# A graph layer on one core: the last two adjacency tiles loaded by row groups, zero products in TensorE's gaps, roots on VectorE, and a new split of PSUM banks

## The chip, the cores and the metric

The kernel runs on one core of a Trainium2 chip. Its time is the device time in microseconds; the median of the runs counts. Profiles are of one execution each, and every time inside one is counted from the start of its span. PE is TensorE, DVE is VectorE, ACT is ScalarE, POOL is GpSimd, and SP is the queue that issues the transfers.

## The reference

`x` is 4096 by 64, `adj` is a 4096 by 4096 matrix of zeros and ones in float32 (64 MB), `weight` is 64 by 64 and `bias` has 64 values.

```
h       = relu(layernorm(x))
support = h @ weight
mask    = adj != 0
rank    = cumsum(mask, axis=1)
deg     = rank[:, -1:]
k       = minimum(deg, 100)
pos     = rank - (deg - k)
w       = mask * where(pos > 0, 0.5 ** (k - pos), 0)
out     = x + w @ support + bias
```

Only a row's last hundred neighbours count, and each weighs half of the next one. So every row needs a running count over its 4096 columns before its weights are known.

## The kernel before

`adj` is worked through in 32 tiles of 128 rows, each 2 MB. Thirty are loaded whole as "rows" (line 307, in units of two tiles): a partition holds one row of 4096 floats in a run of 16 KB. Tile 0 comes in two halves. Tiles 30 and 31 form one unit of kind "columns": a partition holds a quarter of the columns of four rows, so that four row groups and four column quarters are spread over the partitions, and the runs are 4 KB. Tile 31 is two pieces of 128 columns there. Each of the quarter's transfers goes to 32 partitions (line 311):

```
to = tiles[t].rearrange("(q p) (g n) -> q p g n", q=E, g=E)
for q in range(E):
    nc.sync.dma_start(to[q, :, k0:k1, :], quarters[t // HT, t % HT, q, :, k0:k1, :])
```

Each piece passes these steps. `convert` (DVE, line 509) turns floats into bytes, `flip` (DVE, lines 520 and 525) transposes blocks of them, `totals` (PE, 532) counts ones, `split` (ACT, 538) takes two bytes of the counts, `suffix` (PE, 551) adds up what lies behind each block, `clamp` (DVE, 556) subtracts the excess over 100, `place` (PE, 565 and 570) writes into four PSUM banks the exponent of every element, and four `weigh` (ACT, 584) take the exponentials, which are the weights. `aggregate` (PE, 601) multiplies them with the support, 32 products for a unit of two tiles. After each four tiles `drain` (ACT, 611; the last one DVE, 613) adds the bias, `turn_back` (PE, 619) transposes, `finish` (DVE, 626 and 627) adds the two halves to `x`, and `store` (SP, 631) writes out.

Ahead of that stands the layer norm: `turn`, `turned`, `center`, `square`, `relu`, `spread` (PE, 458), `root` (DVE, 462 to 464), `power` (POOL, 469 to 474, three Newton steps for the reciprocal root), `support` (PE, 479), `scale` (DVE, 482), `first` and `second` (ACT and DVE, 489 and 492), which split the support into two summands.

The order on every engine is fixed before the kernel runs. `tasks` lists each step with the engine, what it needs, how long it holds its engine, and a due time from the table `DUE`. `plan` then walks through the tasks and gives each engine's next one by readiness and due time; the kernel issues them in that order, and every engine keeps it. So an engine that stands at a step that isn't ready holds back all behind it. A load of tile t waits for the convert of tile t - 4, since there are four buffers for loaded tiles (`NA`). There are four for converted bytes (`NM`) and four for flipped ones (`NT`).

PSUM's eight banks are divided in `NV, NB`: five for exponents (pool `ps_v`, also used by the layer norm), two for counts (pool `ps_t`: totals, suffix and turn_back take turns), and one for the accumulator (`ps_a`).

`warm` issues products of zeros, which keep PE at work in early gaps. It is called from the loop at the end of the kernel, from line 637 on, where the plan leaves PE idle for more than 700 ns, and no more once `spread` has come.

Of the kernel before, what the change touches and what calls it, by code (L numbers as in the profile page):

```python
# [30 lines left out]
UNITS = [("rows", ((t, 0, 4), (t + 1, 0, 4))) for t in range(0, 30, 2)] + [("columns", ((30, 0, 4), (31, 0, 2), (31, 2, 4)))]  # L31
SPANS = {"rows": 8, "columns": 2}
STEP = {0: 2}
# [3 lines left out]
for u, i in PIECES:  # L37
# [3 lines left out]
DRAINS = [(g, 0, 4, True) for g in range(7)] + [(7, 0, 2, True), (7, 2, 3, True), (7, 3, 4, False)]  # L41
STORES = [(0, 0, 16), (1, 0, 12), (1, 12, 14), (1, 14, 15), (1, 15, 16)]
NA, NM, NT, NW, NV, NB = 4, 4, 4, 2, 5, 2

DUE = {
    "fetch": [-686, -126],
    "load": [724, 583, 273, 792, 448, 655, 939, 650, 1013, 730, -119, 964, 1305, 584, 218, 814, 1129, 955, 149, 993, 40,
    765, 956, 78, 684, 958, 306, 922, 424, 450, 164, 71, 1115, 730],
    "load_rest": [-204],
    "turn": [359, 315, 260, 710, 487, 222, 133, -266],  # L50
    "turned": [-185, -335, 64, -727, -1045, -251, -968, -881],
    "center": [360, -58, 207, -35],
    "square": [-87, -1268, -175, 619],
    "relu": [-239, 514, 1391, -334],
    "spread": [-680, -580, -580, 15],
    "support": [21, 24, 95, 42],
    "scale": [861, -308, -468, -124],
    "root": [844],
    "power": [174],
    "constants": [-220, -1059],  # L60
    "order_of": [1056],
    "count": [1111],
    "counted": [10],
    "first": [-514, -397, -30, -113],
    "second": [-417, 143, 783, 704],
    "convert": [482, 1025, 204, 226, 727, 309, 981, 1114, 367, 687, 1132, 1067, 867, 1749, 1371, 1701, 256, 1583, 1540,
    856, 1257, 1456, 1412, 1612, 1915, 1541, 2485, 1819, 1871, 2184, 1807, 1638, 1616, 2086],
    "flip": [-114, 308, 291, 923, 674, -114, 690, 807, -100, 831, 543, 437, 630, 1887, 1255, 1800, 979, 1228, 961, 744,
    1153, 1971, 1323, 1552, 1990, 1126, 1724, 1289, 2088, 1984, 2223, 1296, 1905, 2123],
    "totals": [-3, 552, -46, 841, 433, 189, 81, 601, 415, -464, -591, 136, 611, 1280, 503, 1008, 578, 335, 987, 424,  # L70
    685, 602, 1305, -158, 1197, 1439, 1190, 839, 1469, 919, 1061, 1251, 1091],
    "split": [761, 727, 1045, 717, 751, 769, -156, 772, 17, 1132, 865, 862, 499, 667, 955, 987, 1510, 1187, 1234, 350,
    1194, 1337, 750, 878, 1289, 1830, 1061, 1369, 1498, 1532, 1176, 1109, 1727],
    "suffix": [183, 405, -150, 111, 631, -317, 930, 770, 128, 167, 1286, 587, 1533, 512, 1005, 852, 704, 676, 956, 1751,
    1680, 1362, 1491, 577, 1388, 1268, 1495, 1814, 1765, 1130, 1431, 1709, 2042],
    "clamp": [321, 347, 443, 415, 222, 598, 567, 424, 121, 506, 857, 749, 466, 653, 638, 701, 1299, 997, 674, -57, 972,
    1295, 1419, 477, 1910, 863, 1576, 1079, 584, 801, 1235, 1277, 1913],
    "place": [-25, 778, 16, 550, 117, -32, 40, -6, 92, 41, -143, 48, 468, -231, -158, 1140, 356, 68, 498, 801, 768,
    1322, 971, 1992, 893, 1057, 834, 1829, 1233, 1823, 1881, 1472, 1293],
    "weigh": [-539, -10, 974, 122, -11, -72, 83, 150, 27, 775, 317, 129, -832, -333, -51, 636, 535, 294, 532, 123, 180,  # L80
    378, 466, -70, 639, 222, 730, 838, 795, 370, 3, 64, 752, 536, 729, 774, 139, 88, 559, 654, 785, 582, 88, 787, 1053,
    118, 807, 706, 489, 825, 591, 69, 761, 655, 427, 704, 340, 743, -9, 457, 789, 281, 1115, 479, 792, 1172, 665, 313,
    1129, 1711, 790, 1140, 1070, 953, 1054, 509, 1453, 384, 1493, 842, 315, 782, 467, 940, 983, 1433, 1265, 954, 1411,
    876, 1666, 1502, 1255, 848, 803, 1220, 1400, 1237, 1021, 1867, 1311, 858, 1342, 1376, 1740, 1425, 1760, 1471, 2210,
    1505, 1441, 1561, 1791, 1838, 1656, 2274, 2036, 1458, 1383, 852, 799, 1464, 848, 1978, 1179, 1428, 1547, 1352, 796,
    2201, 1653, 1588],
    "aggregate": [405, 292, 97, 611, -155, 1241, -31, 842, 332, 334, 1114, 914, 1063, 882, 706, 826, 632, 748, 1116,
    423, 423, 679, 89, 819, 525, 722, 392, 807, 611, 1238, 1392, -269, 1280, 824, 135, 740, 1044, 980, 682, 959, 368,
    650, 826, 977, 447, 432, 945, 564, 860, 911, 943, 1550, 795, 1481, 1191, 503, 690, 693, 824, 516, 1094, 676, 1580,
    2035, 1092, 1330, 876, 1281, 1390, 1259, 1542, 2317, 1637, 1016, 1566, 1168, 1392, 1083, 962, 1526, 1048, 1123,  # L90
    1190, 1017, 661, 1207, 2606, 1891, 1494, 1205, 1663, 1458, 782, 2062, 1503, 2022, 1500, 2071, 2003, 1841, 1219,
    1977, 1613, 827, 1835, 2025, 1748, 1355, 1745, 1953, 2096, 2431, 899, 2009, 1570, 1701, 1819, 1985, 2681, 1641,
    1109, 2260, 2265, 2409, 2272, 1848, 924, 1875],
    "drain": [64, 247, 512, 1185, 1142, 1625, 1534, 1794, 1955, 2201],
    "turn_back": [1333, 1555, 2261, 2462, 2286, 2762, 2419, 1952, 2550, 2777],
    "finish": [403, 912, 821, 1212, 1760, 2467, 1688, 2395, 2803, 2383],
    "store": [10242, 11508, 11343, 11289, 10767],
# [14 lines left out]
def tasks():  # L112
# [36 lines left out]
    task("power", (), POOL, 3, 2600, 2700, [("root",)])  # L149
# [8 lines left out]
    for n, (u, i, k0, k1) in enumerate(LOADS):  # L158
        k = k1 - k0
        due = when[u, i]  # L160
        hold = 622 * k + 20
        task("convert", (n,), DVE, due, hold, hold + 170, [("load", n)], ("b", ("flip", n)))
        hold = 268 * k + (60 if UNITS[u][0] == "rows" else 120)
        o = PIECES.index((u, i))
        task("flip", (n,), DVE, due + 2, hold, hold + 120, [("convert", n)] + ([("place", *PIECES[o - NT])] if o >= NT else []))
    for u, i in PIECES:
        kind, pieces = UNITS[u]
        due, w = when[u, i] + 3, width(u, i)
        task("totals", (u, i), PE, due, 470 * w // 512 + 95, 470 * w // 512 + 315, [("flip", n) for n, part in enumerate(LOADS) if part[:2] == (u, i)], ("t", ("split", u, i)))
        task("split", (u, i), ACT, due + 0.5, 2 * w * 833 // 1000 + 50, 2 * w * 833 // 1000 + 190, [("totals", u, i)])  # L170
        hold = (650 if kind == "rows" else 350) * w // 256
        task("suffix", (u, i), PE, due + 1, hold, hold + 220, [("split", u, i)], ("t", ("clamp", u, i)))
        task("clamp", (u, i), DVE, due + 1.5, w * 1042 // 1000 + 125, w * 1042 // 1000 + 245, [("suffix", u, i), ("counted",)])
        hold = 750 if w == 256 else 650
# [13 lines left out]
    for d, (g, i0, i1, on_act) in enumerate(DRAINS):  # L188
        u = max(u for u in range(U) if any(g * 4 + i0 <= t < g * 4 + i1 for t, _, _ in UNITS[u][1]))
        due = when[u, len(UNITS[u][1]) - 1] + 15  # L190
        k = i1 - i0
        task("drain", (d,), ACT if on_act else DVE, due, 107 * k + 130 if on_act else 134 * k + 125, 107 * k + 270 if on_act else 134 * k + 250, [("aggregate", u, 7)])
        task("turn_back", (d,), PE, due + 1, 109 * k, 109 * k + 230, [("drain", d)], ("t", ("finish", d)))
        task("finish", (d,), DVE, due + 1.5, 2 * (67 * k + 130), 2 * (67 * k + 130) + 60, [("turn_back", d)])
# [7 lines left out]
FREE = 1200, 3400, 4000, 5500, 800  # L202
# [3 lines left out]
def dma_ns(f, args):  # L206
    if f == "fetch":
        return 1250
    u, _, k0, k1 = LOADS[args[0]]
    return (k1 - k0) * (1288 if UNITS[u][0] == "columns" else 1224 if k1 - k0 == 4 else 1247)  # L210


def plan():
# [6 lines left out]
    while kinds:  # L220
# [22 lines left out]
        order.append((at, len(order), hold, engine == PE, f, args))  # L243
    return [o[:1] + o[2:] for o in sorted(order, key=lambda o: o[:2])]
# [3 lines left out]
def kernel(  # L248
# [14 lines left out]
    nc = tc.nc  # L263
# [17 lines left out]
    dpool = ctx.enter_context(tc.tile_pool(name="dpool", bufs=1))  # L281
# [18 lines left out]
    def load(n):  # L300
# [7 lines left out]
        else:  # L308
            to = tiles[t].rearrange("(q p) (g n) -> q p g n", q=E, g=E)
            for q in range(E):  # L310
                nc.sync.dma_start(to[q, :, k0:k1, :], quarters[t // HT, t % HT, q, :, k0:k1, :])
# [42 lines left out]
    make_identity(nc, ident)  # L354
    less = setup.tile([P, H, D], F32, name="less")
# [71 lines left out]
    none = ps_a.tile([P, W], F32, tag="acc", name="none")  # L427

    def warm(n):
        for i in range(n):  # L430
            nc.tensor.matmul(none[:, :2 * P], junk[:, :P], junk, start=True, stop=True)
# [22 lines left out]
    def spread(n):  # L454
        if n == 0:
            pxs["var"] = ps_a.tile([P, W], F32, tag="acc", name="pd")
# [10 lines left out]
    def power():  # L467
        y, t, v = ns["y"], ns["t"], ns["v"]
        nc.gpsimd.tensor_scalar(v, v, -0.5, None, op0=ALU.mult)
        for i in range(3):  # L470
            nc.gpsimd.tensor_tensor(t, y, y, op=ALU.mult)
# [208 lines left out]
```

## Time and profile before

| | |
|---|---|
| median of 3 runs | 200.74 us (199.84 to 201.24) |
| the profiled execution | 200.25 us, of which the span is 198.0 |
| busy in the span | PE 164.3, DVE 152.1, ACT 153.3, POOL 9.9 us |
| mean granted PE clock | 0.914 |
| moved | 68.19 MB read, 1.05 MB written, 350 GB/s over the span |
| products of zeros (line 431) | 20 |
| loads of tiles 30 and 31 (line 311) | 4 of 512 KB, 8 of 256 KB |
| last convert, last exponents, end | 177.3, 188.9 to 191.0, 198.0 us |

Busy times are means over stages with different limits. What counts for an edit is which wait ends last in the stage that it touches, so the views to read are the rate by slices, the chain of waits, and the timeline of the end.

### The profile page before, as it was taken

What the parts mean: (1) busy time and instruction counts of PE and PEld (TensorE: products, weight loads), DVE (VectorE), ACT (ScalarE), POOL (GpSimd) and SP (SyncE); (2) the same over time, 40 slices, a digit from 0 to 9 for tenths busy, and PEclk for the clock granted to TensorE, in tenths of its full rate; (3) what the DMA queues carried; (4) which work ended last, traced back from release to release, by engine and by line L of the source; (5) the groups of instructions that cost most, each with busy time, mean ns of one, the idle gap of its engine ahead of it and who ended that gap; (6) DMA issues with size and microseconds to landing.
All of it is one profiled execution on the core that took longest, in us unless ns stands there. A gap on an engine that the chain in (4) does not pass through costs nothing.

```text
span 198.0 us, 4612 instructions
## 1 busy us (share of the span) xinstructions
PE 164.3 (83%) x2007; PEld 124.3 (63%) x2007; DVE 152.1 (77%) x169; ACT 153.3 (77%) x195; POOL 9.9 (5%) x46
## 2 busy tenths in 40 slices
PE   7899882698965998898988898998988978568992
PEld 5775571386753776676666776785866755445881
DVE  4876869996996988979988689999989845664212
ACT  2863468385938997999999999989999996286650
POOL 7000820000000000000000000000000000000000
PEclk9995599559999999999999999999999996965899
DMA  6999999999999999999999999999999999830020
GB/s 221 405 434 424 440 424 406 437 427 427 427 420 424 422 430 420 427 424 434 424 424 417 430 417 427 427 430 424 430 417 391 199 223 223 243 118 3 0 93 13
DMA packets 6947, 69.52 MB, mean 351 GB/s; under 512 B 1296, under 2 KB 1424, under 8 KB 2960
## 3 DMA queue, kind: packets, MB, share of 16 engines
q1 hardware_dynamic: 6768, 69.21, 88.0%
q8 instruction: 15, 0.25, 0.5%
q10 hardware_dynamic: 160, 0.03, 0.1%
q14 instruction: 4, 0.03, 0.1%
HBM read 68.19 MB, written 1.05 MB: 350 GB/s over the span
## 4 chain that ended last, share of the span: by engine, by line
PE 37%; DMA 22%; DVE 17%; ACT 15%; POOL 3%; issue 3%; SPq 1%; POOLq 0%; ACTq 0%; DVEq 0%
PE acc L601 22%; DMA a_sb<-in_adj_dram 22%; ACT wk L584 12%; DVE m L509 8%; PE ps L551 5%; DVE mt L520 4%; PE v L570 3%; PE v L565 3%; PE tot L532 3%; DVE behind L556 2%; POOL t L473 2%; ACT sums L538 1%; PE po L619 1%; ACT acc_sb L611 1%; DVE wk L482 1%
## 5 line engine op out<-in xcount | busy, mean ns | idle before, releaser
L584 ACT ACTIVATE wk<-v 128x1024 fp32r<-128x1024 uint8 (+1 forms) x132 | 123.0, 1029 | 13.7 <-PE v L570 12.6
L509 DVE TENSOR_SCALAR m<-a_sb 128x4096 uint8<-128x4096 f32 (+1 forms) x34 | 84.0, 2479 | 13.4 <-DMA a_sb<-in_adj_dram 13.4
L601 PE MATMUL acc<-wk,hr 128*128 128x256 f32 x512 | 78.1, 304 | 6.2 <-ACT wk L584 5.4
L601 PEld LDWEIGHTS acc<-wk,hr 128*128 128x128 f32 x512 | 68.6, 203 | 14.6 <-ACT wk L584 7.6
L520 DVE STREAM_TRANSPOSE mt<-m 128x1024 f32<-128x1024 f32 (+1 forms) x31 | 37.1, 1203 | 0.3
L538 ACT ACTIVATE sums<-tot 128x512 f16<-128x512 uint8 (+1 forms) x33 | 20.0, 607 | 14.2 <-PE tot L532 7.8
L556 DVE TENSOR_SCALAR behind<-ps,excess 128x256 f16<-128x256 f32 (+1 forms) x33 | 15.5, 470 | 19.0 <-PE ps L551 17.1
L565 PE MATMUL v<-behind,where 32*128 32x256 f16 (+1 forms) x264 | 16.8, 281 | 12.1 <-DVE behind L556 8.7
L532 PE MATMUL tot<-mt,band 128*32 128x256 f16 (+1 forms) x264 | 14.3, 300 | 4.6 <-DVE mt L520 3.1
L551 PEld LDWEIGHTS <-far_rows 128*128 128x128 f16 x210 | 17.3, 103 | 1.2
L565 PEld LDWEIGHTS <-where 32*128 32x128 f16 x264 | 5.9, 93 | 19.2 <-issue 16.5
L551 PE MATMUL ps<-sums,far_rows 128*128 128x224 f16 (+6 forms) x210 | 17.8, 228 | 0.0
L570 PE MATMUL v<-mt,tri 32*32 32x512 f16 (+1 forms) x528 | 15.3, 413 | 0.0
L551 PE MATMUL ps<-sums,near 128*128 128x256 f16 (+1 forms) x33 | 9.7, 293 | 4.7 <-ACT sums L538 4.6
L532 PEld LDWEIGHTS <-band 128*32 128x32 f16 x264 | 4.4, 97 | 11.4 <-issue 5.3
L570 PEld LDWEIGHTS <-tri 32*32 32x32 f16 x528 | 4.6, 88 | 7.2 <-issue 7.0
L551 PE MATMUL ps<-sums,rest_rows 128*128 128x256 f16 x30 | 8.6, 287 | 0.0
L611 ACT ACTIVATE acc_sb<-acc,bias_sb 128x512 f32<-128x512 f32 (+2 forms) x9 | 5.8, 644 | 2.8 <-PE acc L601 2.7
L551 PEld LDWEIGHTS <-near 128*128 128x128 f16 x33 | 3.5, 105 | 5.6 <-issue 3.4
L458 PEld LDWEIGHTS pd<-ones,wk 128*128 128x128 f32 x32 | 5.0, 234 | 1.8 <-ACT wk L449 1.3
L619 PE MATMUL po<-ident,acc_sb 128*128 128x128 f32 x31 | 5.1, 282 | 1.0 <-ACT acc_sb L611 1.0
L449 ACT ACTIVATE wk<-pc 128x512 f32<-128x512 f32 x4 | 2.4, 600 | 4.6 <-PE pc L446 4.6
(93 smaller groups left out, 87.7 us busy)
## 6 DMA issues: line engine op xcount, KB each, us to landing
a_sb<-in_adj_dram SPq DMA_DIRECT2D x29, 2048.0 KB, 13.8
a_sb<-in_adj_dram SPq DMA_DIRECT2D x2, 1024.0 KB, 8.6
a_sb<-in_adj_dram SPq DMA_DIRECT2D x4, 512.0 KB, 19.1
a_sb<-in_adj_dram SPq DMA_DIRECT2D x8, 256.0 KB, 11.9
xr<-in_x_dram SPq DMA_DIRECT2D x2, 512.0 KB, 3.8
out_dram<-xr SPq DMA_DIRECT2D x1, 512.0 KB, 7.4
out_dram<-xr SPq DMA_DIRECT2D x1, 384.0 KB, 2.3
out_dram<-xr SPq DMA_DIRECT2D x1, 64.0 KB, 1.7
```

The source lines that it names most:

```text
L509: nc.vector.tensor_scalar(m_v, a_v, 0.0, 64.0, op0=ALU.not_equal, op1=ALU.add)
L520: nc.vector.transpose(to.rearrange("p c (h r) -> p h c r", r=SUB)[:, 2 * k0:2 * k1], m_v)
L532: nc.tensor.matmul(tot[SUB * c:SUB * (c + 1), :w], band[:, SUB - 12 - 4 * a:2 * SUB - 12 - 4 * a], masks[u, i][:, c, :w, a], start=(a == 0 ...
L538: nc.scalar.activation(sums8[u, i][:, :, :w], pts.pop((u, i, "n"))[:, :w].bitcast(U8).rearrange("p (i f) -> p f i", f=4)[:, :2, :], AF.Cop ...
L551: nc.tensor.matmul(o, l, m, start=(k == 0), stop=(k == len(todo) - 1), skip_group_check=True)
L556: nc.vector.tensor_scalar(behind[u, i][:, :w], pts.pop((u, i, "s"))[:, :w], excess, float(MAX_NEIGH), op0=ALU.subtract, op1=ALU.min)
L565: nc.tensor.matmul(vs[u, i, j][:, a * w:(a + 1) * w], where[q, a, :], behind[u, i][q, :w], start=(a == 0), stop=False, skip_group_check=True)
L570: nc.tensor.matmul(vs[u, i, j][SUB * c:SUB * (c + 1), :2 * w], tri[q, q], masks[u, i][q, c, :w, :].rearrange("p i a -> p a i"), start=Fals ...
L584: nc.scalar.activation(to, v, AF.Exp, scale=-LN2, bias=-38.0 * LN2)
L601: nc.tensor.matmul(accs[g][:, at:at + 2 * P], hr[:, b, :, :].rearrange("p s d -> p (s d)"), w, start=(k == m == 0), stop=(k == 7 and m == ...
L611: nc.scalar.activation(sums[d][:, :w], accs[g][:, i0 * P:i1 * P], AF.Identity, bias=bias_sb)
L619: nc.tensor.transpose(pts["o", d][:, k, :, :].rearrange("p s d -> p (s d)"), sums[d][:, k * P:(k + 1) * P], ident)
```

## The change

It has several parts. The loads of tiles 30 and 31 become one transfer for each group of rows, over all 128 partitions, eight in all; tile 31 is one piece of 256 columns again, loaded in two steps. Zero products are put in wherever the plan leaves PE idle, up to a limit for the rows streamed in 3.4 us, and go to the accumulator's bank. `power` moves to DVE with nine instructions instead of thirteen. `ps_v` gets six banks and `ps_t` one, and `sums8` two buffers. `turn_back` multiplies with a matrix that adds the two halves, so `finish` is one addition. The last drains are two, of two tiles each. The durations in `tasks` and all of `DUE` are new, and with them the order on every engine.

```diff
-UNITS = [...] + [("columns", ((30, 0, 4), (31, 0, 2), (31, 2, 4)))]
+UNITS = [...] + [("columns", ((30, 0, 4), (31, 0, 4)))]
-STEP = {0: 2}
+STEP = {0: 2, 31: 2}
-DRAINS = [(g, 0, 4, True) for g in range(7)] + [(7, 0, 2, True), (7, 2, 3, True), (7, 3, 4, False)]
-STORES = [(0, 0, 16), (1, 0, 12), (1, 12, 14), (1, 14, 15), (1, 15, 16)]
-NA, NM, NT, NW, NV, NB = 4, 4, 4, 2, 5, 2
+DRAINS = [(g, 0, 4, True) for g in range(7)] + [(7, 0, 2, True), (7, 2, 4, True)]
+STORES = [(0, 0, 16), (1, 0, 12), (1, 12, 14), (1, 14, 16)]
+NA, NM, NT, NW, NV, NB = 4, 4, 4, 2, 6, 1
...
-            to = tiles[t].rearrange("(q p) (g n) -> q p g n", q=E, g=E)
-            for q in range(E):
-                nc.sync.dma_start(to[q, :, k0:k1, :], quarters[t // HT, t % HT, q, :, k0:k1, :])
+            for k in range(k0, k1):
+                nc.sync.dma_start(tiles[t][:, k * N // 4:(k + 1) * N // 4], quarters[t // HT, t % HT, :, :, k, :])
...
+    both = const.tile([P, D], F32, name="both")
+    nc.vector.tensor_add(both, ident[:, :D], ident[:, D:])
...
-    none = ps_a.tile([P, W], F32, tag="acc", name="none")
+    idle = [ps_a.tile([P, W], F32, tag="acc", name="none")]
 
     def warm(n):
-        for i in range(n):
-            nc.tensor.matmul(none[:, :2 * P], junk[:, :P], junk, start=True, stop=True)
+        for i in range(n if idle else 0):
+            at = 0 if accs else 2 * P
+            nc.tensor.matmul(idle[0][:, at:at + 2 * P], junk[:, :P], junk, start=not accs, stop=not accs, skip_group_check=True)
...
         if n == 0:
-            pxs["var"] = ps_a.tile([P, W], F32, tag="acc", name="pd")
+            pxs["var"] = idle[0]
...
-        nc.gpsimd.tensor_scalar(v, v, -0.5, None, op0=ALU.mult)
         for i in range(3):
-            nc.gpsimd.tensor_tensor(t, y, y, op=ALU.mult)
-            nc.gpsimd.tensor_tensor(t, t, v, op=ALU.mult)
-            nc.gpsimd.tensor_scalar(t, t, 1.5, None, op0=ALU.add)
-            nc.gpsimd.tensor_tensor(y, y, t, op=ALU.mult)
+            nc.vector.tensor_tensor(t, y, y, op=ALU.mult)
+            nc.vector.scalar_tensor_tensor(t, v, -0.5, t, op0=ALU.mult, op1=ALU.mult)
+            nc.vector.scalar_tensor_tensor(y, t, 1.5, y, op0=ALU.add, op1=ALU.mult)
...
-            nc.tensor.transpose(pts["o", d][:, k, :, :].rearrange("p s d -> p (s d)"), sums[d][:, k * P:(k + 1) * P], ident)
+            nc.tensor.matmul(pts["o", d][:, k, :], sums[d][:, k * P:(k + 1) * P], both, start=True, stop=True)
...
-        nc.vector.tensor_add(o, po[:, :i1 - i0, 0, :], o)
-        nc.vector.tensor_add(o, po[:, :i1 - i0, 1, :], o)
+        nc.vector.tensor_add(o, pts.pop(("o", d))[:, :i1 - i0, :], o)
...
+    spent, end, result = [], 1200, []
+    for at, hold, engine, f, args in order:
+        idle = 0
+        if engine == PE:
+            recent = sum(rows for when, rows in spent if when > at - 3400)
+            idle = max(0, min(int((at - end) * 0.6) // 110, (3400 - recent) // 256))
+            spent += [(at, rows_of(f, args) + 256 * idle)]
+            end = at + hold
+        result.append((at, idle, f, args))
+    return result
```

`quarters` is `adj.rearrange("(r g p t) (q n) -> r t q p g n", r=H, g=E, t=HT, q=E)` in both kernels.

## The prediction

> **What bounds the kernel now.** I read the page's slices first, then the table of stretches, the DMA issues by tile, the chain of waits and last the timeline of the end. The slices:
>
> ```profile
> DMA  6999999999999999999999999999999999830020
> GB/s 221 405 434 424 440 424 406 437 427 427 427 420 424 422 430 420 427 424 434 424 424 417 430 417 427 427 430 424 430 417 391 199 223 223 243 118 3 0 93 13
> ```
>
> A slice is 4.95 us. The DMA engines are full from the second slice to the 34th, but what they move falls from about 425 to about 210 GB/s in the 32nd, near 153 us. The stretches (PE, PEld, DVE, ACT and POOL busy, clock, DMA share, GB/s) say the same:
>
> ```profile
> 120.00:140.00 20.00, 18.98 (x253) 14.79 (x253) 19.36 (x18) 19.24 (x24) 0.00 (x0) 1.00 1.01 428
> 152.00:154.00 2.00, 1.49 (x25) 0.96 (x24) 1.90 (x3) 2.00 (x4) 0.00 (x0) 1.00 1.08 285
> 154.00:163.14 9.14, 7.57 (x106) 6.17 (x103) 5.90 (x4) 9.11 (x12) 0.00 (x0) 1.00 1.00 209
> 163.14:177.30 14.16, 9.88 (x109) 7.38 (x109) 8.26 (x11) 7.75 (x11) 0.00 (x0) 0.79 0.80 205
> ```
>
> Full engines at half the rate: the 12 transfers of tiles 30 and 31 (line 311) follow the row tiles (line 307). 285 GB/s as a mix of 425 and 209 puts the last row tile's landing near 152.7 us, so I take 152.8. ACT, busy throughout until then, runs dry afterwards. The chain of waits closes with it:
>
> ```profile
> 148.19 21.58 DMA a_sb<-in_adj_dram
> 169.79 7.38 DMA a_sb<-in_adj_dram
> 177.20 0.05 DVEq L509
> 177.25 0.05 issue
> 177.30 1.37 DVE m L509
> 178.67 0.37 DVE behind L556
> 179.08 0.61 PE v L565 x8
> ```
>
> So the end is set by the landing of the last half tile (177.2 us) and 20.8 us of work behind it. Up to 153 us the row stream sets the pace: 2.10 MB at 425 GB/s is 4.93 us a tile. ACT needs, by its timeline, 4 exponents of 0.965 (six in 5.80), a split of 0.62 and a quarter of a drain of 0.70, 4.66 us together. It keeps up and is no later bound.
>
> [...] 209 for the 32-partition loads, 425 for the others. [...] each of its large patterns starts with 32 or 128 partitions on both sides[...] and its DMA share is 1.00. [...] the clock is 1.00 to 164 us, then 0.79 and 0.69 when PE waits for loads.
>
> **The change part by part.** *The loads.* The destination is now 128 partitions by 1024 floats[...]. But the source is indexed as `quarters[r, t, :, :, k, :]`, with dimensions q = 4 (a step of 1024 columns), p = 32 (a step of 16 rows) and n = 1024. q and p have unrelated steps and can't merge, so the outermost size is 4 on the source and 128 on the destination[...] each of the 8 transfers runs on the same four engines and the other twelve idle. One engine's rate from the row stream is 425/16 = 26.6 GB/s; four give 106. One transfer of 524 KB then takes 4.93 us instead of about 2.5 now, and eight take 39.4. Bounds: engines that ran alone at the densest stretch's 487/16 = 30.4 GB/s would need 34.5 us; 4-KB runs at the 385 GB/s that the stretch with the x fetches has (24.1 each), 43.6. I take 39.4: row tiles and column tiles go through the same queue. The last half lands at 152.8 + 39.4 + 0.5 (to the semaphore, an estimate) = 192.7 us against 177.2, 15.5 later. If all 16 engines served it, at 425, it would land at 152.8 + 9.9 + 0.5 = 163.2.
>
> *Behind the landing.* DVE's new order is: convert of 31's second half, clamp of 30, four flips, finish of drain 6, clamp of 31. So tile 30's clamp is queued behind a convert that waits for the landing, and everything after it repeats per tile. Step by step, in us:
> - convert 1.37, with clamp 30 starting 1.27 after it as now: 194.0, ending at 194.5;
> - turn_back 6 shares the one count bank with clamp 30 and stands ahead of place 30 on PE: 8 passes of 0.126 (the support row's rate), 1.1 with its wait: 195.6;
> - place 30 to the first exponent, 1.29 now at half clock: 196.9;
> - totals 31 during that exponent, its split behind it (1.02 + 0.6) at 198.5, while 12 aggregate products that wait on nothing run at half clock, 0.235 each: 200.3; suffix 0.9 and clamp 31 0.5: 201.7. ACT has finished tile 30's exponents by 201.5;
> - 8 aggregate products, then place 31: 203.4; four exponents of 1.02: 207.5;
> - the last 8 products at 0.116 and a wait: 208.6; two drains 0.8, two products 0.4, finish 0.3 and waits of 0.2: 210.3; last store to the end, 2.66 as now: 213.0.
>
> That is 20.3 us behind the landing, against 20.8. The last columns are stored once instead of twice, and tile 31 is one piece of 256 columns instead of two of 128; these gain what the second serial pass costs. An error of 3 us either way is left in this sum.
>
> *Edits that lie beside the stream.* All of these act under a DMA queue that was full; their cover is the 39 us in which four engines deliver the last two tiles, when every other engine catches up. With that cover gone (loads at full rate) they count, and I price that with the rival.
> - The roots move from POOL to DVE: POOL's steps, 19.88 to 26.5 us with one of 2.65, become 9 DVE instructions of about 0.19 (the three root rows), 1.7 us. They stand ahead of the convert of tile 2, which waits some 1.4 us longer; three loads are queued on SP's queue by then, so the stream doesn't notice. The scales come after that convert, near 26 us, about when POOL was done; the gain is 0 to 4.
> - Zero products: 58 instead of 20; 38 more of 0.107 to 0.215, 4 to 8 us of PE, in gaps of the first 45 us and near the end. They keep the clock in the stretches at 0.5, and a product that overruns a gap delays ACT by 0.2. Net 0 to a gain of 2.
> - Six banks for exponents, one for counts: totals and suffix wait until split and clamp have read. Per tile: totals 0.41, split 0.60, suffix 0.75, clamp 0.48 and four handovers of about 0.15, 2.8 us; a wait for one exponent adds 1.0. That fits in 4.93. Behind a waiting suffix on PE stand place and aggregate, and ACT waits for place. Cost 0, up to 2.6 per tile when clamp stands behind a convert.
> - Turn_back through a sum of both halves: 8 DVE additions of 0.42 fewer, 3.4 us, hidden by DVE's idle time. SP issues 8 loads for 12 and 4 stores for 5, 0.32 each, hidden by the queue.
>
> Sum: the span of 198.0 becomes 213.0. The profiled execution took 200.25 (2.25 around the span), so 215.3; this execution lies 0.5 below the median of 200.74. I forecast **215.3 us**, +7%.
>
> **The rivals.** *A, all 16 engines serve the new loads (faster).* [...] For it: nothing in the trace shows a transfer on fewer engines, and 128 partitions move at 425. [...] The landing would be 163.2, and ACT's remaining work decides: after 154 us it is 26.8 busy us in the stretches, so the last exponent ends at 180.8, less about 3 from the earlier start; then 5.5 to the end: 183.3 span, 185.6 us. The point from which it decides is 8 engines: 8 times 26.6 is what the loads have now.
> *B, the one count bank becomes the bound on top.* If clamp waits out a whole convert, the loop is 2.8 + 2.6 = 5.4 us, 0.47 above 4.93, and thirty tiles end 14 us later: 229. For it: DVE already waits 11.0 us for suffix. Against it: in the new order clamp stands directly behind each convert, and flip and convert of the next tile (3.9) give the loop time.
> *C, the four transfers of a tile run on different engines,* so that about eight are busy at once: the loads stay at some 20 us and only the shorter ending shows, 199 to 202.
>
> **How the numbers follow.** Forecast 0.82, A 0.12, B 0.04, C 0.02. The forecast's own bounds: 152.8 + 34.5 + 0.5 + 17.5 + 2.25 = 207.6 to 152.8 + 43.6 + 0.5 + 23.3 + 2.25 = 222.5; I give 207 to 223, which leaves A, B, C and little else out. Faster by over 1% is A, 0.12; within 1% is C, 0.02; slower is the forecast and B, 0.86. A measurement of this kernel can tell about 1% from no change.
>
> **What would show it.** Right: GB/s near 106 and a DMA share near 0.25 from 153 us on, issue to landing of the loads of tile 31 up to 40 us, the last convert starting near 192.7, and ACT idle for over 15 us before it. The row stream still ends near 153. Wrong: GB/s near 425 and a DMA share of 1 until 163 us (A); about 210 (C); or a row stream below 415 GB/s with clamp and suffix in the waits (B). If loads and landing are right and the end isn't, the sum behind the landing failed.

## The result and the profile after

The changed kernel took **220.23 us** (median of 4 runs, 218.61 to 221.32); the kernel before, beside it, 200.51 (199.84 to 201.24). The ratio is **1.0976** (95% interval 1.0883 to 1.1069): slower by 19.7 us. The forecast was 215.3, with a range of 207 to 223. The profiled execution took 218.61 us, of which the span is 216.9. A kernel's executions fall into a faster and a slower group: medians below are of all of them and ratios of the faster ones alone, and three of the profiles below are of slower ones (the change with the loads of before, the last unit as rows, eight outermost).

The slices of the changed kernel (5.42 us each) show where the time went:

```profile
PEclk9889996996999999999999999999999955755699
DMA  6999999999999999999999999999522224220100
GB/s 233 419 434 432 423 416 429 393 429 426 426 419 429 423 429 423 432 420 423 432 417 426 423 429 420 435 426 423 223 106 103 103 103 179 104 102 14 73 3 26
```

Up to the 28th slice (152 us) the row tiles stream at about 425 GB/s, as before. The 29th is mixed. From the 30th to the 36th the DMA engines are busy for a quarter and move 102 to 106, but for one slice of 179. The kernel before showed busy engines at 199 to 243 while the same tiles were loaded. The stretches of the changed kernel (length, busy us of PE, PEld, DVE, ACT and POOL with counts, granted clock, DMA share, GB/s):

```profile
120.00:140.00 20.00, 19.05 (x273) 14.70 (x272) 16.55 (x13) 19.22 (x24) 0.00 (x0) 1.00 1.00 424
160.00:170.00 10.00, 6.90 (x95) 5.25 (x80) 2.62 (x3) 8.20 (x10) 0.00 (x0) 1.00 0.26 103
170.00:180.00 10.00, 1.62 (x26) 0.77 (x26) 4.00 (x4) 0.33 (x1) 0.00 (x0) 0.66 0.26 105
182.00:184.00 2.00, 1.10 (x7) 0.61 (x5) 0.00 (x0) 1.53 (x3) 0.00 (x0) 0.65 0.73 297
190.00:194.00 4.00, 0.00 (x0) 0.00 (x0) 0.00 (x0) 0.00 (x0) 0.00 (x0) 0.50 0.25 102
```

A share of 0.25 of 16 engines is four, at 103/4 = 25.8 GB/s each. In the last of these stretches no engine computes at all. The one exception, 182 to 184 us, is a store of 524,288 B: (297 - 103) times 2 us is 388 KB, three quarters of it, which fits the twelve idle engines taking their shares at once.

The chain of waits of the changed kernel (start, us, what) closes so:

```profile
162.01 4.89 SPq L327
166.94 4.88 SPq L327
171.87 23.88 DMA a_sb<-in_adj_dram
195.84 1.30 DVE m L526
197.65 1.94 PE po L638 x8
...
206.12 4.47 PE acc L618 x36
211.20 1.21 PE acc L618 x8
```

The last half tile lands at 195.75 us, against 177.20 before, and 21.15 us of work follow, against 20.8. So all but 0.35 us of the loss in the span stands ahead of the landing. The timeline behind it (start, us, instruction, idle time before it and what ended that):

```profile
195.84 1.30 DVE L526 TENSOR_SCALAR m<-a_sb 128x2048 uint8<-128x2048 f32 x1 [8.86 <-DMA a_sb<-in_adj_dram]
197.03 0.47 DVE L573 TENSOR_SCALAR behind<-ps,excess 128x256 f16<-128x256 f32 x1
197.65 1.94 PE L638 MATMUL po<-both,acc_sb 128*128 128x64 f32 x8 [14.55 <-DVE behind L573]
200.87 1.02 ACT L601 ACTIVATE wk<-v 128x1024 fp32r<-128x1024 uint8 x1 [14.97 <-PE v L587]
206.21 3.77 ACT L601 ACTIVATE wk<-v 128x1024 fp32r<-128x1024 uint8 x4 [1.07 <-PE v L587]
211.20 1.21 PE L618 MATMUL acc<-wk,hr 128*128 128x256 f32 x8 [0.62 <-ACT acc_sb L630]
214.12 0.29 DVE L644 TENSOR_TENSOR xr<-po,xr 128x128 f32<-128x128 f32 x1 [0.99 <-PE po L638]
```

Tile 30's clamp (line 573) does stand behind tile 31's convert, as the plan's order said; PE and ACT have waited some 15 us for it.

### The profile page after: what moved, and what is told of

It is laid out like the page before. It is cut to its first block, busy times and chain, and to the rows that moved or that the text cites. A ratio compares the mean times of both kernels' runs of the same rounds, so it can differ in the third digit from the quotient of the medians.

```text
span 216.9 us, 4657 instructions
## 1 busy us (share of the span) xinstructions
PE 167.7 (77%) x2041; PEld 127.3 (59%) x2041; DVE 149.8 (69%) x166; ACT 153.8 (71%) x190; POOL 4.1 (2%) x33
## 4 chain that ended last, share of the span: by engine, by line
PE 42%; DVE 18%; ACT 17%; DMA 11%; issue 5%; SPq 5%; POOL 1%; ACTq 0%; POOLq 0%; DVEq 0%
PE acc L618 19%; ACT wk L601 12%; DMA a_sb<-in_adj_dram 11%; DVE m L526 7%; PE ps L568 5%; SPq L327 5%; PE po L638 4%; DVE mt L537 4%; ACT sums L555 4%; PE tot L549 3%; PE v L587 3%; DVE behind L573 3%; PE v L582 2%; PE none L477 2%; PE px L457 2%
## 5 line engine op out<-in xcount | busy, mean ns | idle before, releaser
L601 ACT ACTIVATE wk<-v 128x1024 fp32r<-128x1024 uint8 x128 | 123.7, 1066 | 36.3 <-PE v L587 35.8
L573 DVE TENSOR_SCALAR behind<-ps,excess 128x256 f16<-128x256 f32 x32 | 15.2, 476 | 20.4 <-PE ps L568 20.1
L582 PE MATMUL v<-behind,where 32*128 32x256 f16 x256 | 13.9, 289 | 12.2 <-DVE behind L573 11.7
L555 ACT ACTIVATE sums<-tot 128x512 f16<-128x512 uint8 x32 | 19.6, 614 | 4.9 <-PE tot L549 4.8
L638 PE MATMUL po<-both,acc_sb 128*128 128x64 f32 x64 | 9.7, 297 | 16.2 <-DVE behind L573 15.2
L638 PEld LDWEIGHTS po<-both,acc_sb 128*128 128x128 f32 x64 | 8.6, 208 | 18.1 <-issue 14.8
L549 PE MATMUL tot<-mt,band 128*32 128x256 f16 x256 | 13.7, 292 | 5.8 <-DVE behind L573 4.6
L587 PE MATMUL v<-mt,tri 32*32 32x512 f16 x512 | 15.1, 421 | 0.0
L582 PEld LDWEIGHTS <-where 32*128 32x128 f16 x256 | 4.4, 93 | 17.2 <-issue 14.8
L568 PE MATMUL ps<-sums,near 128*128 128x256 f16 x32 | 9.3, 290 | 3.9 <-ACT sums L555 2.4
L450 PE MATMUL none<-junk 128*128 128x256 bf16 x41 | 8.0, 338 | 1.4 <-DVE junk L339 1.1
```

The source lines that it names most:

```text
L450: nc.tensor.matmul(idle[0][:, at:at + 2 * P], junk[:, :P], junk, start=not accs, stop=not accs, skip_group_check=True)
L549: nc.tensor.matmul(tot[SUB * c:SUB * (c + 1), :w], band[:, SUB - 12 - 4 * a:2 * SUB - 12 - 4 * a], masks[u, i][:, c, :w, a], start=(a == 0 ...
L555: nc.scalar.activation(sums8[u, i][:, :, :w], pts.pop((u, i, "n"))[:, :w].bitcast(U8).rearrange("p (i f) -> p f i", f=4)[:, :2, :], AF.Cop ...
L568: nc.tensor.matmul(o, l, m, start=(k == 0), stop=(k == len(todo) - 1), skip_group_check=True)
L573: nc.vector.tensor_scalar(behind[u, i][:, :w], pts.pop((u, i, "s"))[:, :w], excess, float(MAX_NEIGH), op0=ALU.subtract, op1=ALU.min)
L582: nc.tensor.matmul(vs[u, i, j][:, a * w:(a + 1) * w], where[q, a, :], behind[u, i][q, :w], start=(a == 0), stop=False, skip_group_check=True)
```

## The experiments

The theory is the forecast's, where it was the author's assumption: a transfer whose source starts with a dimension of four runs on four engines, and that alone makes the loss. The first four kernels ran beside one kernel before (199.15 us), the next four beside another (199.32), the last two pairs beside 199.33 and 199.10. Ratios are to the kernel before of the same group. Wherever the rows of the source are taken in another order, a partition holds another row, or another quarter of a row, than the later steps assume, so the output of the last two tiles is not the reference's; the work is all done, and such a kernel is a measurement only.

**The change with the loads of before.**

```diff
-            for k in range(k0, k1):
-                nc.sync.dma_start(tiles[t][:, k * N // 4:(k + 1) * N // 4], quarters[t // HT, t % HT, :, :, k, :])
+            to = tiles[t].rearrange("(q p) (g n) -> q p g n", q=E, g=E)
+            for q in range(E):
+                nc.sync.dma_start(to[q, :, k0:k1, :], quarters[t // HT, t % HT, q, :, k0:k1, :])
```

> The changed kernel with the loads of tiles 30 and 31 put back to the form before (each transfer to 32 partitions, source and destination both starting with 32; 12 transfers), all else as changed. Theory (the loss is the source's outermost size of 4, which leaves four engines): about 209 GB/s with a DMA share of 1 after 153 us, the last half landing near 174, then the 21.2 us that the changed kernel has behind its landing: span 195, 197 us, somewhat below the kernel before. Rival (the single count bank, the zero products or the new order cost time as well): 204 us or more, with the loads landing as early.

Measured: 199.78 us, ratio 0.9994 (0.9957 to 1.0032). The loads are back at the rate of before:

```profile
154.00:160.00 6.00, 5.95 (x81) 5.07 (x80) 3.10 (x3) 4.85 (x7) 0.00 (x0) 1.00 1.00 208
```

Putting them back takes all of the loss away, and what is left of the change is worth nothing measurable beside such loads. In the profiled execution (202.25 us) the last convert started at 179.3 us, some 5 later than I had put it; its last transfers were issued only up to 170.2 us. What held them is not shown.

**The kernel before with the new loads alone.** The reverse edit, in the kernel before.

> The kernel before with only the new loads (one transfer for each row group over 128 partitions, source starting with 4), tile 31 still in two pieces. Theory: about 103 GB/s and a DMA share of 0.26 after 153 us, the last half landing near 195.5, then the 20.8 us behind it: span 216.5, 218.8 us, so this edit alone makes the whole loss. Rival (other edits carry part of it): 212 us or less.

Measured: 217.99 us, ratio 1.0992 (1.0931 to 1.1053). Its slices and its stretch from 160 us:

```profile
GB/s 241 427 435 415 424 423 424 433 427 418 430 417 427 433 418 430 424 418 430 430 421 427 421 424 430 421 424 424 226 99 106 103 103 177 103 102 19 0 86 12
160.00:170.00 10.00, 8.00 (x94) 6.67 (x91) 3.64 (x5) 8.33 (x10) 0.00 (x0) 1.00 0.26 105
```

The same rate, the same share, the last convert at 195.7. The load edit makes the loss alone, and without it the loss is gone.

**The same loads with another outermost dimension.** Four transfers per tile, the same 128 partitions, the same runs of 4 KB; only the order of the source's dimensions differs, 32 rows outermost and the four column quarters second.

```diff
-    quarters = adj.rearrange("(r g p t) (q n) -> r t q p g n", r=H, g=E, t=HT, q=E)
+    mixed = adj.rearrange("(r g p t) (q n) -> r t p q g n", r=H, g=E, t=HT, q=E)
...
-                nc.sync.dma_start(tiles[t][:, k * N // 4:(k + 1) * N // 4], quarters[t // HT, t % HT, :, :, k, :])
+                nc.sync.dma_start(tiles[t][:, k * N // 4:(k + 1) * N // 4], mixed[t // HT, t % HT, :, :, k, :])
```

> The changed kernel with the source of the eight loads indexed with its 32 rows outermost and the 4 quarters second; destination, bytes and runs of 4 KB stay. A partition then gets another quarter of another row than the later steps assume, so tiles 30 and 31 are computed from permuted data; no work is left out. Theory (the outermost size decides how many engines serve a transfer, and 32 and 128 give 16): over 400 GB/s until 163 us, last half landing near 163.5, and ACT's remaining work then sets the end: 183 to 188 us. Rival (a source of two dimensions that don't merge is slow in any order, or 4-KB runs are): 103 GB/s again and 219 us.

Measured: **188.31 us**, ratio 0.9477 (0.9423 to 0.9531). Its stretches:

```profile
154.00:160.00 6.00, 5.95 (x79) 5.08 (x78) 5.70 (x4) 4.85 (x7) 0.00 (x0) 1.00 0.99 398
170.00:180.00 10.00, 9.18 (x118) 7.68 (x117) 2.65 (x7) 10.00 (x13) 0.00 (x0) 1.00 0.11 41
```

With the partitions and the length of the runs held fixed, the order of the source's dimensions alone takes the rate from 103 to 398 GB/s. The end is then set by ACT, busy for 10.00 of 10 us, as rival A reasoned for a kernel whose loads reach all engines. The walk through memory changes with the order too. But with four outermost the share was 0.26, and each busy engine moved 25.8 GB/s, close to the 26.6 of the row stream: fewer engines were busy (0.26 against 0.99), and those that were did not move much less.

**A dose between the two: eight outermost.**

```diff
+    eighths = adj.rearrange("(r b a t) (k n) -> r t a b k n", r=H, b=16, a=8, k=E)
```

> The changed kernel with the source of the eight loads in two dimensions that don't merge, 8 outermost and 16 second (128 rows in another order, one column quarter each); 128 partitions, 4-KB runs and bytes stay. Tiles 30 and 31 are computed from permuted data; no work is left out. Theory (the outermost size decides): eight engines, 206 GB/s and a DMA share near 0.5 after 153 us, last half landing near 174, then 21 us: span 195, 197 us; between the 103 GB/s of size 4 and the 400 of size 32. Rival (any outermost size under 16 gives one fixed slow form): 103 GB/s and 219 us.

Measured: 201.79 us, ratio 1.0105 (1.0056 to 1.0154), some 5 us above my 197. Its stretches:

```profile
154.00:160.00 6.00, 5.33 (x74) 4.46 (x72) 5.32 (x6) 5.67 (x8) 0.00 (x0) 1.00 0.79 240
160.00:170.00 10.00, 8.90 (x124) 6.77 (x123) 5.11 (x4) 8.85 (x12) 0.00 (x0) 1.00 0.57 227
170.00:176.00 6.00, 3.02 (x41) 1.72 (x39) 4.31 (x5) 1.81 (x2) 0.00 (x0) 0.80 0.52 209
```

The first stretch still holds the end of the row stream, and the second a part of the first store, issued at 164.7 us. In the third the loads run alone: half of the engines are busy, at 209 GB/s. So 4, 8 and 32 outermost give 103, 209 and 398 GB/s at shares of 0.26, 0.52 and 0.99, which is about four, eight and sixteen of the 16 engines. Other sizes were not run. The miss of 5 us stays open: in the profiled execution (204.39 us) the last load of a row tile was issued 2.5 us later than in the changed kernel (145.2 against 142.7), but that execution is itself 2.6 above the median.

**Quarters in another order.** 32 partitions a transfer, as before, but 256 KB each and alternating between quarters.

```diff
-            for k in range(k0, k1):
-                nc.sync.dma_start(tiles[t][:, k * N // 4:(k + 1) * N // 4], quarters[t // HT, t % HT, :, :, k, :])
+            to = tiles[t].rearrange("(q p) (g n) -> q p g n", q=E, g=E)
+            for k in range(k0, k1, 2):
+                for q in (0, 2, 1, 3):
+                    nc.sync.dma_start(to[q, :, k:k + 2, :], quarters[t // HT, t % HT, q, :, k:k + 2, :])
```

> The changed kernel with tiles 30 and 31 loaded in 16 transfers of 256 KB to 32 partitions each, in the order of quarters 0, 2, 1, 3, so that neighbours in the queue go to different halves of the partitions; everything computed. Theory one[...]: 209 GB/s as with the loads before, about 199 us. Theory two[...]: 300 GB/s or more, the last half landing before 168, 188 to 192 us.

Measured: 198.02 us, ratio 0.9932 (0.9901 to 0.9962). Its stretch:

```profile
154.00:160.00 6.00, 5.95 (x79) 5.07 (x79) 3.55 (x4) 4.85 (x7) 0.00 (x0) 1.00 0.99 208
```

208 GB/s at a share of 0.99, as with quarters in order (208 at 1.00): transfers that alternate between the halves of the partitions did not add up here. Why a transfer to 32 partitions keeps all engines busy at half of the row stream's 424 GB/s is not shown.

**The last unit as rows.** Tiles 30 and 31 are loaded and worked like the other thirty; everything is computed.

```diff
-UNITS = [...] + [("columns", ((30, 0, 4), (31, 0, 4)))]
+UNITS = [...] + [("rows", ((30, 0, 4), (31, 0, 4)))]
```

> The changed kernel with tiles 30 and 31 as an ordinary unit of rows (16-KB rows, tile 31 in two halves of 2048 columns), everything computed. Theory: the row rate of 425 GB/s holds to the end, last half landing near 163.3; all 32 aggregate products of the last unit wait for its last exponent instead of the last 8, some 2.8 us more than with rows outermost: 187 to 191 us, faster than both kernels. Rival (the single count bank or the new order keeps the gain back, or the serial 32 products cost more than the slow loads of before): 197 us or more.

Measured: **193.16 us**, ratio 0.9647 (0.9569 to 0.9725), faster than both kernels, but above the 187 to 191 that I expected. The loads ran at 419 GB/s; the miss is at the end. The chains of waits, of the kernel with rows outermost, of this one (its execution of 194.06 us), and of the one with few zero products below:

```profile
181.82 1.22 PE acc L618 x8
```

```profile
181.51 5.55 PE acc L618 x32
```

```profile
182.18 4.04 PE acc L618 x32
```

A unit of kind "columns" lets its products start with each exponent and leaves 8 for the end. A unit of kind "rows" has all 32 wait for the last exponent: 4.3 us more on the path here. Of these, 2.8 were in the expectation; they are the price of 24 more products at the rate of the third line. The other 1.5 is the clock, as the stretches of these two kernels show (granted clock third from the end):

```profile
181.50:187.00 5.50, 5.49 (x34) 5.49 (x34) 0.00 (x0) 0.00 (x0) 0.00 (x0) 0.69 0.00 0
181.50:187.00 5.50, 4.43 (x36) 4.29 (x36) 0.29 (x1) 0.92 (x3) 0.00 (x0) 1.00 0.00 0
```

It is 0.69 in the kernel before with that unit as rows (below) as well. Why it falls in these and not in the one with few zero products is not shown: PE had stood idle ahead of the products for 2.65 us in the second line's kernel and for 2.66 in the third's.

**Two banks for counts, and few zero products, on that kernel.**

```diff
-NA, NM, NT, NW, NV, NB = 4, 4, 4, 2, 6, 1
+NA, NM, NT, NW, NV, NB = 4, 4, 4, 2, 5, 2
```

> The changed kernel with its last unit in rows (as in the run that loads tiles 30 and 31 as rows), and five banks for exponents with two for counts, as before the change; the order is planned anew with them. Theory of the prediction (a single count bank costs nothing, since 2.8 us a tile fit in 4.93): 193 us, within 1% of that run. Rival (the single bank delays place and ACT): 190 us or less. Third (the sixth exponent bank is what keeps ACT fed): 196 us or more.

Measured: 193.06 us, ratio 0.9669 (0.9611 to 0.9727), the same as with one bank. Nor did the single bank of the changed kernel lengthen the wait that rival B feared. What DVE's clamp waited for suffix from 30 to 155 us (us, times, longest), in the kernel before and in the changed one:

```profile
DVE behind L556 <- PE ps L551: 11.0, 13, 2.7
```

```profile
DVE behind L573 <- PE ps L568: 10.2, 15, 1.9
```

```diff
-        warm(spare)
+        warm(spare if at < 10500 else 0)
```

> The changed kernel with its last unit in rows, and zero products only before the first center (18 of 60); the order is the same. Theory of the prediction (they gain up to 2 us by the clock): 193 to 195 us, with the clock at 0.5 in more of the first 45 us. Rival (they stand in ACT's way and cost time): 191 us or less.

Measured: 196.47 us, ratio 0.9747 (0.9681 to 0.9814). The ratio differs by 0.0100 from that of the kernel with all zero products (0.9647), or by 2.0 us; with the half-widths of both added in squares that is about 0 to 4.0, so this pair alone doesn't settle it.

**What the other edits are worth uncovered.** The kernel before with the loads of the kernel with rows outermost; and that kernel with few zero products (the edit just shown). What the first text calls four row groups are the four column quarters.

> The kernel before with the new load loop alone, and its source taken with the 32 rows outermost and the four row groups second, so the last two tiles hold permuted rows and the output differs there. The question is what the other edits (roots on DVE, zero products, banks, turn_back, drains) are worth once slow loads no longer cover them. Theory one, they gain a little, as the prediction's bounds of 0 to 4 us for the roots and 0 to 2 for the zero products: 189 to 194 us, against 188.3 for the changed kernel with the same loads. Theory two, they are worth nothing even uncovered: 187.5 to 189. Theory three, the single count bank costs up to 2.6 us a tile somewhere: below 187. Loads at 400 to 420 GB/s from 154 us on in every case.

> The changed kernel with the 32 rows outermost in the new loads (188.3 us, with permuted rows in the last two tiles, so the output differs there), and zero products issued only ahead of 10.5 us of the plan, 18 instead of 60. With those loads the other edits together were worth 3.5 us (191.8 without them), and ACT had done 94.1 us of work between 50 and 150 us, against 90.6 without them. Theory one, the zero products make that gain, by keeping the clock in the first 50 us: 190.5 to 193, clock below 0.9 in 0 to 50 us, ACT some 2 to 4 us behind by 150. Theory two, they don't and it comes from the order, the banks or the ending: 187.5 to 189.5.

Measured: 191.78 us (ratio 0.9643, 0.9570 to 0.9716) and 192.85 us (0.9693, 0.9611 to 0.9774), against 188.31 (0.9477, up to 0.9531) with all the edits. The stretches of the three, in the order all edits, few zero products, none of the edits:

```profile
0.00:50.00 50.00, 39.57 (x370) 28.04 (x371) 39.76 (x73) 29.34 (x42) 4.09 (x33) 0.93 0.96 397
50.00:150.00 100.00, 91.63 (x1286) 71.24 (x1285) 89.34 (x70) 94.12 (x114) 0.00 (x0) 1.00 1.01 426
```

```profile
0.00:50.00 50.00, 35.94 (x336) 26.81 (x337) 39.97 (x74) 29.54 (x42) 4.08 (x33) 0.89 0.97 402
50.00:150.00 100.00, 91.95 (x1266) 71.26 (x1265) 87.36 (x69) 92.31 (x111) 0.00 (x0) 0.97 1.01 425
```

```profile
0.00:50.00 50.00, 39.05 (x370) 28.32 (x370) 39.31 (x65) 29.89 (x43) 9.98 (x46) 0.83 0.97 403
50.00:150.00 100.00, 89.52 (x1191) 68.86 (x1188) 87.19 (x72) 90.60 (x109) 0.00 (x0) 0.97 1.01 425
```

With these full-rate loads the zero products are worth **4.3 us** (58 of them in the trace, against 18): the two ratios differ by 0.0216, of 199; their half-widths, 0.0054 and 0.0081, added in squares make that 2.4 to 6.2. The pair above, 0 to 4.0, lies lower and overlaps. Without them nothing of the other edits' gain is left (192.85 against 191.78); the drains and turn_back were not tried alone.

ACT sets the end there. Between 50 and 150 us it does 94.12 us of work with them and 92.31 without, and its last seven exponents, first with them and then without, stand 3.6 us apart, as the two spans do (187.5 and 191.0):

```profile
174.20 6.58 ACT L601 ACTIVATE wk<-v 128x1024 fp32r<-128x1024 uint8 x7
```

```profile
177.76 6.58 ACT L601 ACTIVATE wk<-v 128x1024 fp32r<-128x1024 uint8 x7
```

The clock is 0.93 against 0.89 up to 50 us, and 1.00 against 0.97 from there to 150. That the clock is the way is argued from these columns, not shown by itself. A part of theory one of the second of these runs failed: by 150 us ACT had fallen behind by 1.8 us, not 2 to 4.

**The last unit as rows in the kernel before.** `UNITS` as above, and tile 31 in one piece loaded in two steps.

> The kernel before with one edit: its last unit is loaded and worked as rows like the other thirty tiles, tile 31 in one piece loaded in two steps. Everything is computed. The changed kernel with that unit took 193.2 us. Theory one (the other edits gain a little once uncovered): 193.5 to 198. Theory two (they are worth nothing): 192 to 194. In both the loads run at 415 to 425 GB/s to their end near 163 us, and the kernel before gains at least 3 us by this edit alone.

Measured: 194.20 us, ratio 0.9738 (0.9698 to 0.9778). That one edit gains 5.1 us; with the other edits of the change it was 0.9647, and the intervals overlap a little, so what the other edits add here is not clear.

**The store that meets the loads.**

```diff
-STORES = [(0, 0, 16), (1, 0, 12), (1, 12, 14), (1, 14, 16)]
+STORES = [(1, 0, 12), (0, 0, 16), (1, 12, 14), (1, 14, 16)]
```

> The changed kernel with its first two stores in the other order on the issue queue. The first store (512 KB) goes out at 176.8 us there, while four engines still deliver the last loads; now it stands behind a store that waits for drain 6 and so for the last landing. Everything is computed. Theory one, the store's share on the four engines delayed the landing, by 131 KB at 25.8 GB/s for each engine, 1.3 us: last convert starts near 194.5 (195.8 in the changed kernel) and no rise of the rate near 183 us; the time 218.5 to 220 against 220.2. Theory two, it cost nothing: last convert at 195.5 to 196.1, with the time the same. In both the store adds at most 1 us behind the landing, since 16 engines take it.

Measured: 219.54 us, ratio 1.1035 (1.0959 to 1.1110), the last convert at 196.16, and the rate still rises near 183 us (299 GB/s). The edit changed the plan and not the queue: the three quarters of a 524,288-B store moved near 183 us here too, and its issue stands at 177.2 as in the changed kernel at 176.8. The loop at the end of the kernel ties PE, DVE, ACT and POOL to the plan's order, and not SP. So this run is a repeat of the changed kernel. What the store costs can be read from the traces all the same (below, under the landing): nothing ahead of the landing.

## Why the prediction was right, point by point

Size and sign were right, and by the mechanism that it gave. In its own steps:

| step | predicted | measured |
|---|---|---|
| row stream ends | 152.8 us | 152 to 156, below |
| rate of the new loads | 106 GB/s, share 0.25 | 103, share 0.26 |
| last convert starts | 192.7 | 195.84 |
| clamp 30 ends, after the landing | +1.8 | +1.75 |
| turn_back 6 ends | +2.9 | +3.8 |
| first exponent of 30 starts | +4.2 | +5.1 |
| 12 products end | +7.6 | +8.3 |
| clamp 31 ends | +9.0 | +9.2 |
| exponents of 31 end | +14.8 | +14.2 |
| last 8 products end | +15.9 | +16.7 |
| last addition ends | +17.6 | +18.7 |
| end of the span | +20.3 | +21.15 |
| time around the span | 2.25 | 1.71 |

The profiled 218.61 lies 3.3 above 215.3: 3.1 from the landing, 0.8 from the work behind it, less 0.5 around the span. The median lies 4.9 above.

*The landing.* Four engines was right; it was the author's assumption, since no pattern of the kernel before could show it, and the doses of 4, 8 and 32 confirm it (shares of 0.26, 0.52 and 0.99). The DMA records of the changed kernel say the same: a row tile is complete in sixteen parts, each of the eight new loads in four. The 3.1 us have three parts. The converts of tile 30 and of tile 31's two halves each waited for their landing:

```profile
175.53 2.43 DVE L526 TENSOR_SCALAR m<-a_sb 128x4096 uint8<-128x4096 f32 x1 [12.76 <-DMA a_sb<-in_adj_dram]
185.68 1.30 DVE L526 TENSOR_SCALAR m<-a_sb 128x2048 uint8<-128x2048 f32 x1 [6.13 <-DMA a_sb<-in_adj_dram]
195.84 1.30 DVE L526 TENSOR_SCALAR m<-a_sb 128x2048 uint8<-128x2048 f32 x1 [8.86 <-DMA a_sb<-in_adj_dram]
```

They stand 10.15 and 10.16 us apart, for two transfers each, so one takes 5.08 us, and the eight take 40.6 where I had 39.4: one of the four engines gave 25.8 GB/s, between the 26.6 of the row stream that I took and the 24.1 of my upper bound. That is 1.2. The last transfer is recorded as complete at 195.03 us, so 0.8 passed until the convert, where I had 0.5. The rest, 1.6, is the handover. I let the row stream end at 152.8 on every engine, but it ran out one engine after another:

```profile
154.00:155.00 1.00, 1.00 (x28) 0.66 (x13) 1.00 (x1) 0.67 (x2) 0.00 (x0) 1.00 0.63 238
155.00:156.00 1.00, 1.00 (x11) 0.96 (x10) 1.00 (x1) 1.00 (x3) 0.00 (x0) 1.00 0.39 156
```

Counted back from 195.03 by eight transfers of 5.08, the last of the four engines took up the new loads at 154.4.

The store paid for none of this, against theory one of the last experiment: it moved between the first two of these three converts, and their distance is that of the other two. In the trace's DMA records twelve of its sixteen parts are complete at 183.4 to 183.5 us. The other four are complete at 195.2 to 196.4, behind the last load, whose four parts are complete at 193.7 to 195.0. That fits four engines which work off their transfers in the order of issue.

*Behind the landing.* The order of the steps held to the last, and the errors cancel in part. Turn_back was priced at 0.126 us for each of 8 passes, a rate at full clock; PE had stood idle, the clock was 0.50 before it, and it took 1.94 us where I had 1.1 with its wait. The turn_back before it, at a clock of 1.00, shows the rate that I took:

```profile
152.41 1.08 PE po L638 x8
```

The prediction took half-clock durations for the products and missed them one step earlier. The exponents of tile 31 came 0.6 earlier than thought. And the last 8 products stood 0.62 us at a drain of the other half of the same accumulator, where the sum had about 0.2 for a wait.

*The edits beside the stream.* That they cost nothing under the cover of the slow loads held: with the loads of before the rest of the change gives 0.9994, and the load edit alone gives the whole loss. The single count bank showed no cost with full-rate loads either. The roots gained no time for the scales: on DVE they end at 26.1 us against 26.5 on POOL, and the plan puts a convert of 2.64 us between them and the scales, which start at 28.51 against 26.54. The zero products were mis-sized: 0 to 2 us where uncovered, and 4.3 was measured. The prediction's reading of the clock, "1.00 to 164 us", holds for the first 10 us and from 50 us on; in the kernel before it was 0.71 to 0.77 between 10 and 50 us, with no zero products there, and in the changed kernel 0.83 to 1.00, with 39 of its 58.

*The rivals.* A had the mechanism of a full-rate kernel right (ACT's remaining work decides) but not this kernel's loads; 185.6 was its price, and 188.3 was measured where the loads were made to reach all engines. Its 5.5 us from the last exponent to the end were 6.7. B fell with the row stream, which held 424 GB/s, and with the two count banks; C fell with the share of 0.25 and the four parts of each load, which end 5.08 us after those of the one before: eight transfers on the same four engines, one after the other.

## What to carry to other kernels

Before a transfer is widened over partitions, look at the outermost dimension of its source: it went from 32 to 4 here, with the partitions from 32 to 128, and the rate went from 209 to 103 GB/s, while putting the longer dimension first gave 398 with the same partitions and the same length of runs. (That order delivers other rows and quarters to each partition, so the steps behind must be made for it; no kernel here did that.) Where a special layout for the last tiles needs slow loads, price the plain layout too; here that was 5 us faster with one edit. Edits that look worthless under a full queue may only be covered: all edits beside the loads together gained nothing measurable until the loads were fast, and then the zero products were worth 4.3 us.

## What the runs showed of the hardware that I had not expected

The transfers on four engines also held the queue that issues them, for a median of 4.88 us each, against 0.32 for the loads of before. The tile view lists the issues of the loads (count, then min, median and max in ns, first and last start). Of the kernel before, the changed kernel, and the one with rows outermost:

```profile
L311 SPq DMA_DIRECT2D a_sb<-in_adj_dram x12: 311/323/432, 146.9 to 169.8; - x12
```

```profile
L327 SPq DMA_DIRECT2D a_sb<-in_adj_dram x8: 531/4882/8054, 146.8 to 171.9; - x8
```

```profile
L327 SPq DMA_DIRECT2D a_sb<-in_adj_dram x8: 534/590/977, 145.9 to 157.4; - x8
```

4.88 us is about what one such transfer takes on four engines (524,288 B at 103 GB/s is 5.1), so the queue seems to move at the pace of the engines; with eight engines the median was 1.53 us. Nothing stood behind these loads here but stores with time to spare. What it costs where other loads stand behind them no run here shows.
